# Weights' loads moved, the first lists' stores on another queue, and an addition in place of identity products, in a graph network of four layers

## The chip, the cores and the metric

The kernel runs on one core of a Trainium2 chip. A core has five engines with an instruction stream each: PE (TensorE, matrix products), DVE (VectorE), ACT (ScalarE), POOL (GpSimd) and SP (SyncE, which here only starts DMAs). Every stream is worked off in its written order. DMAs are started by SP and by POOL; sixteen DMA engines move the data. The metric is the device time of one execution in microseconds, as the median of several runs; it was 3134.76 us before (three runs, 3123.56 to 3135.57).

## The reference

Eight batches of a graph with 2048 nodes and 128 features go through four layers over one adjacency matrix (about 17 neighbours a node; the lists have room for 40). Layers 0 and 2 are attention with eight heads of 16, then a feed-forward part; layers 1 and 3 are graph attention with one score per edge:

```python
# layers 0 and 2
scores = jnp.einsum('bnhd,bmhd->bhnm', Q, K) / jnp.sqrt(HEAD_DIM)
scores = jnp.where(adj == 0, -jnp.inf, scores)
x = layer_norm(h + softmax(scores) @ V @ Wo + bo)
x = layer_norm(x + relu(x @ W1 + b1) @ W2 + b2)
# layers 1 and 3
e = leaky_relu(s_i[:, :, None] + s_j[:, None, :])
x = layer_norm(softmax(where(adj == 0, -inf, e)) @ (x @ W) + x)
```

All is in float32. The softmax runs over a node's neighbours only, and the kernel uses that.

## The kernel before, in words

**Tiling.** The nodes are cut into 32 units of 64 nodes. For each layer a *table* lies in memory: one row for each node, with keys and values (attention) or projected features (graph attention) of all eight batches. For each unit the kernel gathers the rows of all its edges, nine gathers of 128 rows, in five steps (two gathers in a step, one in the last), into one of six `kv` buffers. In an attention layer PE spreads each node's query over its edges (`qe`, L1484), DVE multiplies it with the gathered keys (L1496) and sums by head (L1503), ACT takes the exponential, POOL (sometimes DVE) weighs the values (L1522), and PE adds up by node (L1550). Then follow the output product, the norms, the feed-forward part, and the projection of the new features into the next layer's table.

**The start.** Three things run side by side. *Table 0*: `load` (L1188) brings features of four units at a time from memory into a `kv` buffer, `project` (L1280) multiplies by `Wkv` on PE (`ps_p`, L1295), ACT or DVE copies into one of three row buffers, and two DMAs store a unit's rows (L1343). No gather of layer 0 starts before the whole table is stored. *The lists*: `block_list` (L996) reads 128 rows of the adjacency, and DVE finds each node's neighbours in order; `unit_list` (L1076) then makes, for each unit, the list that says which node sits in which slot. ACT writes one-hot columns into a `hot` buffer (three passes, L1104 to L1108), PE multiplies with them so that each slot receives its node's neighbours, degree and offset (`ps_l`, L1117), and a second product with the identity adds the slot's own number in the same accumulation (L1124, the constant `place`). DVE picks from this the neighbour (L1133 to L1151), ACT writes the gather's indices, and the `hot` buffer is stored to memory as `hots[u]` (L1174), from where every layer's `fetch` (L1216) reads it again (L1230), into one of the same three `hot` buffers. *Weights*: `fill` (L909) loads each weight (L915); bias columns are loaded one element to a partition. The list of a unit leads its use by `LEAD`, twelve units of five steps.

**Order.** Nothing here is ordered by hand. `Plan` (L574) gets each operation with an assumed cost, the engines that may do it, what it reads and writes, and a key that says how soon it is due; a list scheduler replays this with a fixed number of buffers for each kind of tile and writes out one order per engine. A layer's keys start at `n * STRIDE`; weights have the key `n * STRIDE - 900`, the first `Wkv` -3000, the features for table 0 `u - 1500`, lists `10 * i - LEAD`. What an operation waits for at run time is what stands before it on its own engine, and the data and buffers it needs. DMAs of SP pass through eight completion counters in turn, so that a DMA also waits for the eighth one before it on this queue.

Of the kernel before, what the change touches and what calls it, by code (L numbers as in the profile page):

```python
# [9 lines left out]
F32 = mybir.dt.float32  # L10
# [5 lines left out]
ALU = mybir.AluOpType  # L16
# [724 lines left out]
class Sparse:  # L741
# [15 lines left out]
    def __init__(self, ctx, tc, x, xt, adj, w, out):  # L757
        self.tc, self.nc, self.w, self.xt_in, self.out = tc, tc.nc, w, xt, out
        self.B, self.N, _ = x.shape
        self.NB = self.N // P  # L760
        self.NU = self.N // UNIT
        self.HB = self.B // 2

        def pool(name, **kw):
            return ctx.enter_context(tc.tile_pool(name=name, **kw))

        self.nc.scalar.preload_act_table_set("natural_log_exp_and_others")
        self.const = pool("const", bufs=1)
        self.dram = pool("dram", bufs=1, space=DRAM)
        self.plan = Plan(self.nc)  # L770
        self.op, self.cell = self.plan.op, self.plan.cell
        for tag, bufs in SBUF_BUFS.items():
            self.plan.pool(tag, pool(f"sb_{tag}", bufs=bufs), bufs, tag in BY_KEY)
        for tag, bufs in PSUM_BUFS.items():
            self.plan.pool(tag, pool(f"ps_{tag}", bufs=bufs, space=PSUM), bufs)

        self.constants()
        self.weights_at = [Cell() for _ in LAYERS]
        self.keys_at = Cell()
        self.gates = {}  # L780
        self.layers = [
            self.mha_weights(n) if kind is MHA else self.gat_weights(n)
            for n, kind in enumerate(LAYERS)
        ]


        self.tables = [
            self.dram.tile([self.N, self.B * (2 * P if kind is MHA else P + 1)], F32, name=f"table_{n}")
            for n, kind in enumerate(LAYERS)
        ]  # L790
        self.table = [Cell() for _ in LAYERS]

# [23 lines left out]
    def constants(self):  # L816
# [23 lines left out]
                allow_small_or_imprecise_dtypes=True,  # L840
            )
        self.rank = ramp("rank", [P, DEG], [[1, DEG]])
        self.place = const.tile([P, TG, 2, DEG + 2], F32, name="place")
        nc.gpsimd.memset(self.place, 0.0)
        for j in range(2):
            nc.gpsimd.iota(
                self.place[:, :, j, DEG],
                pattern=[[P, TG]],
                base=0,
                channel_multiplier=1,  # L850
                allow_small_or_imprecise_dtypes=True,
            )
        nc.gpsimd.iota(
            self.place[:, TG - 1, 1, DEG : DEG + 1],
            pattern=[[1, 1]],
            base=GS - 1,
            channel_multiplier=-1,
            allow_small_or_imprecise_dtypes=True,
        )
        self.place = self.place.rearrange("p t j c -> p t (j c)")  # L860
        self.target = ramp("target", [P, GROUP], [[1, GROUP]], base=1)
        self.falling = const.tile([P, self.N], F32, name="falling")
        nc.gpsimd.iota(
# [45 lines left out]
    def fill(self, n, *pairs, at=None):  # L909

        for t, a in pairs:

            def start(e, t=t, a=a):
                with self.nc.allow_non_contiguous_dma(reason="a small array, once"):
                    e.dma_start(out=t, in_=a)  # L915

            self.op({"SP": 0.45}, start, -3000 if at else n * STRIDE - 900, joins=[at or self.weights_at[n]], dma=P * P * 4)

    def column(self, n, name, width=1):
        t = self.const.tile([P, width], F32, name=f"{name}_{n}")  # L920
# [3 lines left out]
    def mha_weights(self, n):  # L924
        const, w = self.const, self.w[n]
        d = {}
        for name, shape in (("Wq", [P, P]), ("Wkv", [P, 2 * P]), ("Wo", [P, P]), ("W1", [P, FFN])):
            d[name] = const.tile(shape, F32, name=f"{name}_{n}")
        d["W2"] = const.tile([P, FFN // P, P], F32, name=f"W2_{n}")
        self.fill(  # L930
            n, (d["Wkv"][:, 0:P], w["Wk"]), (d["Wkv"][:, P : 2 * P], w["Wv"]), at=None if n else self.keys_at
        )
        self.fill(
            n,
            (d["Wq"], w["Wq"]),
            (d["Wo"], w["Wo"]),
            (d["W1"], w["W1"]),
            (d["W2"], w["W2"].rearrange("(c p) m -> p c m", p=P)),
        )
        d["b1"] = self.column(n, "b1", FFN // P)  # L940
        for name in ("bo", "ln1_g", "ln1_b", "b2", "ln2_g", "ln2_b"):
            d[name] = self.column(n, name)
        return d
# [132 lines left out]
    def unit_list(self, u, p, block_aux, key):  # L1076
# [37 lines left out]
        def parts(e):  # L1114
            for t in range(TG):
# [3 lines left out]
                    lhsT=hot.tile[:, t * P : (t + 1) * P],  # L1119
                    rhs=aux.tile.rearrange("p j c -> p (j c)"),  # L1120
                    start=True,
                    stop=False,
                )
                e.matmul(out, lhsT=self.ident, rhs=self.place[:, t], start=False, stop=True)  # L1124

        op({"PE": 1.6}, parts, key, reads=[hot, aux], writes=[ps_l])
        rank = cell("rank_e", [P, TG, 2])
        pick = cell("pick", [P, TG, 2, DEG])
        shape = [P, TG, 2, DEG]


        def sources(e):
            e.tensor_tensor(  # L1133
                pick.tile,
                self.rank.unsqueeze(1).unsqueeze(1).to_broadcast(shape),
# [2 lines left out]
            )  # L1138
            e.tensor_tensor(pick.tile, pick.tile, ps_l.tile[:, :, :, 0:DEG], ALU.mult)

        op({"DVE": 1.2}, sources, key + 0.4, reads=[ps_l], writes=[pick])

        def ones(e):
            shape = [P, TG, 2, GROUP]
# [12 lines left out]
        def indices(e):  # L1157
# [12 lines left out]

        op({"ACT": 1.2}, indices, key - 2, reads=[rank, ps_l], writes=[self.idx_at[u], both])
        op(
            {"SP": 0.45},
            lambda e: e.dma_start(out=self.hots[u], in_=hot.tile),  # L1174
            key,
            reads=[hot],
# [39 lines left out]
    def fetch(self, n, u, key):  # L1216
# [3 lines left out]
            {"SP": 0.45},  # L1220
            lambda e: e.dma_start(out=x.tile, in_=self.xd[u] if n else self.xt_in[u]),
            key,
            reads=[self.x_at[u]] if n else [],
            writes=[x],
            dma=P * CH * 4,
        )
# [53 lines left out]
    def project(self, n, u, x, key, of=None, shares=()):  # L1280
# [6 lines left out]
        for v in range(2):  # L1287
# [12 lines left out]

            self.op({"PE": 1.1 if mha else 0.7}, products, key, reads=[x, self.keys_at if n == 0 else self.weights_at[n]], writes=[ps], holds=[rows], shares=shares)
            if n == 0:
                self.gates[u] = ps
            if mha:
                self.op(
                    {"ACT": 0.6, "DVE": 0.65} if n == 0 else {"ACT": 0.6},
# [33 lines left out]
        def store(e):  # L1340
# [2 lines left out]
                e.dma_start(out=self.tables[n][nodes, hf * half : (hf + 1) * half], in_=rows.tile[part])  # L1343

        self.op(
            {"SP": 0.9} if n else {"SP": 0.9, "POOL": 1.3}, store, key, reads=[rows], joins=[self.table[n]], dma=P * hb * width * 4
        )

    def norm(self, r, key):
# [502 lines left out]
    def run(self, adj):  # L1852
# [6 lines left out]
                self.load(u, ring)  # L1859
        for i in range(self.NB):  # L1860
            self.block_list(adj, i)
        for n, kind in enumerate(LAYERS):
            if kind is MHA:
                self.attention(n)
            else:
                self.graph(n)
        self.plan.issue()

    def failed(self):
# [72 lines left out]
```

## Time and profile before

| | before |
|---|---|
| median of three runs | 3134.76 us |
| the profiled execution, its own time | 3401.39 us |
| its span | 3399.6 us |
| PE busy / mean granted clock | 2640.6 us (78%) / 0.854 |
| DVE busy | 2190.5 us (64%) |
| ACT busy | 1381.2 us (41%) |
| POOL busy | 2130.8 us (63%) |
| DMA | 1088 MB, mean 320 GB/s |

The profiled execution is slower than the timed ones; times inside it are to be compared with its own span. Busy time says little alone, because the layers have different limits: layer 0 lasts until about 1190 us of the span, layer 1 until about 1870, layer 2 until about 2720. In what follows, an instruction is named by its line, engine, and the tiles it writes and reads (`kv<-qe,kv`); in a timeline the bracket gives the idle time before it and what ended it. The "granted clock" is the share of full speed that PE had.

### The profile page before, as it was taken

What the parts mean: (1) busy time and instruction counts of PE and PEld (TensorE: products, weight loads), DVE (VectorE), ACT (ScalarE), POOL (GpSimd) and SP (SyncE); (2) the same over time, 40 slices, a digit from 0 to 9 for tenths busy, and PEclk for the clock granted to TensorE, in tenths of its full rate; (3) what the DMA queues carried; (4) which work ended last, traced back from release to release, by engine and by line L of the source; (5) the groups of instructions that cost most, each with busy time, mean ns of one, the idle gap of its engine ahead of it and who ended that gap; (6) DMA issues with size and microseconds to landing.
All of it is one profiled execution on the core that took longest, in us unless ns stands there. A gap on an engine that the chain in (4) does not pass through costs nothing.

```text
span 3399.6 us, 69398 instructions
## 1 busy us (share of the span) xinstructions
PE 2640.6 (78%) x26600; PEld 1609.8 (47%) x26600; DVE 2190.5 (64%) x3384; ACT 1381.2 (41%) x4753; POOL 2130.8 (63%) x1452
## 2 busy tenths in 40 slices
PE   6877878888888758778886788888888866777775
PEld 5744444444433336666665333334333335556554
DVE  3778988987887713333333989889988833444434
ACT  3534544545444333333434244444444442333223
POOL 0157877877888834444552878888878835555442
PEclk8778988998999878888888889999999986777676
DMA  7868989988898859998997999999999949899885
GB/s 259 318 236 349 360 313 368 353 335 331 341 344 331 307 196 321 328 335 308 331 341 229 370 340 381 393 367 377 379 356 358 374 166 325 309 320 318 289 281 161
DMA packets 271637, 1088.01 MB, mean 320 GB/s; under 512 B 41217, under 2 KB 59905, under 8 KB 199393
## 3 DMA queue, kind: packets, MB, share of 16 engines
q0 software_dynamic: 166048, 861.26, 67.6%
q1 hardware_dynamic: 105248, 222.23, 18.6%
q8 instruction: 213, 3.49, 0.4%
q14 instruction: 128, 1.04, 0.1%
HBM read 1031.29 MB, written 99.75 MB: 333 GB/s over the span
## 4 chain that ended last, share of the span: by engine, by line
PE 29%; DMA 13%; DVE 11%; issue 11%; POOL 5%; another core or an unknown queue 4%; ACT 3%; ACTq 0%; SPq 0%; DVEq 0%; POOLq 0%
DMA kv<-table,idx 12%; PE acc L1773 6%; DVE kv L1496 5%; PE acc_q L1773 5%; PE ps_c L1262 3%; POOL kv L1522 3%; PE qe L1484 3%; PE ps_te L1651 2%; PE acc L1550 2%; POOL kv L1411 2%; PE ps_p L1295 2%; DVE s L1503 2%; PE ps_t L1250 1%; ACT junk L1358 1%
## 5 line engine op out<-in xcount | busy, mean ns | idle before, releaser
L1411 POOL DMA_INDIRECT kv<-table,idx x1152 | 1180.0, 1024 | 1118.1 <-issue 346.7
L1522 POOL TENSOR_TENSOR kv<-kv 128x2048 f32<-128x2048 f32 (+1 forms) x264 | 943.0, 3583 | 100.8 <-ACT kv L1513 95.2
L1496 DVE TENSOR_TENSOR kv<-qe,kv 128x2048 f32<-128x2048 f32 (+1 forms) x320 | 663.0, 2072 | 156.7 <-DMA kv<-table,idx 110.4
L1503 DVE TENSOR_REDUCE s<-kv 128x128 f32<-128x2048 f32 (+1 forms) x320 | 660.0, 2063 | 7.7
L1484 PE MATMUL qe<-q_sb,hot 32*128 32x512 f32 (+1 forms) x2304 | 398.3, 697 | 170.1 <-DVE kv L1496 155.6
L1773 PE MATMUL acc<-kv,w 128*32 128x128 f32 x5120 | 300.4, 336 | 160.1 <-issue 90.3
L1550 PE MATMUL acc<-kv,hot 128*32 128x512 f32 x2560 | 362.6, 644 | 48.1 <-POOL kv L1522 41.7
L1746 DVE TENSOR_TENSOR w<-hot,e 128x512 f32<-128x512 f32 (+1 forms) x384 | 222.7, 600 | 247.4 <-ACT e L1736 85.3
L1773 PE MATMUL acc_q<-kv,w 128*32 128x128 f32 x5120 | 268.0, 321 | 82.5 <-issue 64.4
L1773 PEld LDWEIGHTS acc<-kv,w 128*32 128x32 f32 x5120 | 190.3, 133 | 245.5 <-issue 156.3
L1513 ACT ACTIVATE kv<-s 128x128 f32<-128x128 f32 (+1 forms) x320 | 95.7, 299 | 406.4 <-DVE s L1503 285.4
L1773 PEld LDWEIGHTS acc_q<-kv,w 128*32 128x32 f32 x5120 | 179.4, 127 | 147.7 <-issue 112.0
L1484 PEld LDWEIGHTS qe<-q_sb,hot 32*128 32x128 f32 (+1 forms) x2304 | 106.8, 197 | 291.3 <-DVE kv L1496 217.6
L1358 ACT ACTIVATE junk<-ps_c,eps 128x128 f32<-128x128 f32 x512 | 187.7, 367 | 113.1 <-PE ps_c L1262 94.7
L1736 ACT ACTIVATE e<-e 128x16 f32<-128x16 f32 (+1 forms) x320 | 66.6, 212 | 316.2 <-DVE e L1731 169.7
L1550 PEld LDWEIGHTS sums<-kv,hot 128*32 128x32 f32 x2560 | 87.7, 116 | 210.8 <-issue 203.8
L1380 ACT ACTIVATE normed<-ps_c,rstd 128x128 f32<-128x128 f32 x512 | 163.4, 366 | 2.4
L1272 PE MATMUL ps_f<-x,W 128*128 128x512 f32 x256 | 148.8, 669 | 18.5 <-ACT x L1397 11.1
L1262 PE MATMUL ps_c<-centre,r 128*128 128x128 f32 x1024 | 148.5, 290 | 18.3 <-DVE kv L1522 9.5
L1262 PEld LDWEIGHTS ps_c<-centre,r 128*128 128x128 f32 x1024 | 127.3, 196 | 71.0 <-DVE r L1587 31.8
L1358 ACT ACTIVATE junk<-r,eps 128x128 f32<-128x128 f32 x256 | 103.2, 403 | 121.1 <-DVE r L1822 92.9
L1250 PE MATMUL ps_t<-ident,normed 128*128 128x128 f32 x640 | 128.1, 329 | 27.5 <-DVE kv L1522 12.1
(156 smaller groups left out, 3992.9 us busy)
## 6 DMA issues: line engine op xcount, KB each, us to landing
hot<-hots SPq DMA_DIRECT2D x128, 480.0 KB
table<-trows SPq DMA_DIRECT2D x126, 256.0 KB
xd<-xnew SPq DMA_DIRECT2D x96, 256.0 KB
x<-xd SPq DMA_DIRECT2D x96, 256.0 KB
kv<-table,idx POOLq DMA_INDIRECT x1152
table<-trows SPq DMA_DIRECT2D x128, 129.0 KB
kv<-adj_dram SPq DMA_DIRECT2D x16, 1024.0 KB
hots<-hot SPq DMA_DIRECT2D x32, 480.0 KB
```

The lines of the kernel that those rows point to most:

```text
L1250: e.transpose(ps.tile[:, b * P : (b + 1) * P], flat(x.tile)[:, b * P : (b + 1) * P], self.ident)
L1262: e.matmul(ps.tile[:, cols], lhsT=flat(x.tile)[:, cols], rhs=self.centre, start=True, stop=True)
L1358: e.activation(self.junk, flat(r.tile)[:, b * P : (b + 1) * P], AF.Square, bias=self.eps, scale=P**-0.5, accum_out=var.tile[:, b : b + 1],)
L1380: lambda e, b=b: e.activation(normed.tile[:, b, :], flat(r.tile)[:, b * P : (b + 1) * P], AF.Copy, scale=rstd.tile[:, b : b + 1],),
L1411: e.indirect_dma_start(out=rows(kv.tile, j), out_offset=None, in_=self.tables[n], in_offset=bass.IndirectOffsetOnAxis(ap=self.idx[:, u, co ...
L1484: e.matmul(qe.tile[:, j, hf, :], lhsT=hot.tile[rows, t * P : (t + 1) * P], rhs=q.tile[rows, :], start=True, stop=True,)
L1496: e.tensor_tensor(k, qe.tile[:, 0:tiles].rearrange("p j h c -> p (j h) c"), k, ALU.mult)
L1503: e.tensor_reduce(s.tile[:, 0 : tiles * heads].rearrange("p (q c) -> p q c", q=2 * tiles), k, axis=mybir.AxisListType.X, op=ALU.add,)
L1522: e.tensor_tensor(v, v, w.unsqueeze(3).to_broadcast([P, 2 * tiles, heads // 2, HD]), ALU.mult)
L1550: e.matmul(out[rows, :], lhsT=hot.tile[:, col : col + GROUP], rhs=rhs[:, 2 * (j % tiles) + hf, :], start=(t == 0), stop=(t == TG - 1),)
L1746: e.tensor_tensor(w.tile[:, j : j + tiles], oh[:, j : j + tiles].unsqueeze(2).to_broadcast(shape), e8.tile[:, 0:tiles].unsqueeze(3).to_bro ...
L1773: e.matmul(acc()[rows, b * P : (b + 1) * P], lhsT=w.tile[:, j, hf * hb + b, :], rhs=both_rows(kv)[:, j % tiles, hf * hb + b, 0:P], start=F ...
```

## The change

The change has four parts.

1. *Weights.* Only `Wkv` of layer 0 is asked for at the start. The other weights of layer 0 read a *gate*: they cannot be planned before the projections of unit 16 are done, those of layer 1 before unit 24's, those of later layers before unit 8 of an earlier layer is stored. The features for layer 0's queries wait for unit 20. `gates` holds cells that no longer keep a tile alive.
2. *Lists' stores.* The `hots` store of the first twelve units goes to POOL's DMA queue; later ones stay on SP's.
3. *Table stores of layer 0.* All on SP; POOL may no longer take them.
4. *Slots' numbers.* `place` shrinks from 84 to 2 columns a tile; the second product with the identity is gone, and DVE adds `place` to one column of `ps_l` in PSUM, ahead of its other work on the list.

```diff
-        self.layers = [
-            self.mha_weights(n) if kind is MHA else self.gat_weights(n)
-            for n, kind in enumerate(LAYERS)
-        ]
+        self.gate = self.keys_at
+        keys = self.const.tile([P, 2 * P], F32, name="Wkv_0")
+        self.fill(0, (keys[:, 0:P], w[0]["Wk"]), (keys[:, P : 2 * P], w[0]["Wv"]), at=self.keys_at)
+        self.layers = [{"Wkv": keys}]
...
-        self.place = const.tile([P, TG, 2, DEG + 2], F32, name="place")
-        nc.gpsimd.memset(self.place, 0.0)
+        self.place = const.tile([P, TG, 2], F32, name="place")
...
-            self.op({"SP": 0.45}, start, -3000 if at else n * STRIDE - 900, joins=[at or self.weights_at[n]], dma=P * P * 4)
+            self.op(
+                {"SP": 0.45},
+                start,
+                -3000 if at else n * STRIDE - 900,
+                reads=[] if at else [self.gate],
+                joins=[at or self.weights_at[n]],
+                dma=P * P * 4,
+            )
...
                     start=True,
-                    stop=False,
+                    stop=True,
                 )
-                e.matmul(out, lhsT=self.ident, rhs=self.place[:, t], start=False, stop=True)
-        op({"PE": 1.6}, parts, key, reads=[hot, aux], writes=[ps_l])
+        op({"PE": 0.8}, parts, key, reads=[hot, aux], writes=[ps_l])
...
         def sources(e):
+            e.tensor_tensor(ps_l.tile[:, :, :, DEG], ps_l.tile[:, :, :, DEG], self.place, ALU.add)
...
-        op({"DVE": 1.2}, sources, key + 0.4, reads=[ps_l], writes=[pick])
+        op({"DVE": 1.3}, sources, key + 0.4, writes=[pick, ps_l])
...
         op(
-            {"SP": 0.45},
+            {"POOL": 0.75} if u < LEAD // TG else {"SP": 0.45},
             lambda e: e.dma_start(out=self.hots[u], in_=hot.tile),
...
-            reads=[self.x_at[u]] if n else [],
+            reads=[self.x_at[u] if n else self.gates[20]],
...
             if n == 0:
-                self.gates[u] = ps
+                self.gates[u] = Cell()
+                self.gates[u].writers = list(ps.writers)
...
-            {"SP": 0.9} if n else {"SP": 0.9, "POOL": 1.3}, store, key, reads=[rows], joins=[self.table[n]], dma=P * hb * width * 4
+            {"SP": 0.9}, store, key, reads=[rows], joins=[self.table[n]], dma=P * hb * width * 4
...
         for i in range(self.NB):
             self.block_list(adj, i)
+        self.gate = self.gates[16]
+        self.layers[0] = self.mha_weights(0)
+        self.gate = self.gates[24]
         for n, kind in enumerate(LAYERS):
+            if n + 1 < len(LAYERS):
+                more = self.mha_weights if LAYERS[n + 1] is MHA else self.gat_weights
+                self.layers.append(more(n + 1))
             if kind is MHA:
                 self.attention(n)
             else:
                 self.graph(n)
+            self.gate = self.x_at[8]
         self.plan.issue()
```

In the order that the planner writes for the changed kernel, SP's first table stores stand right after the first loads of features and adjacency; layer 0's other weights stand among the stores of about the 16th to 19th unit, layer 1's about five units later; unit 0's list is loaded right after the last table store; and eight lists' stores stand in POOL's stream ahead of the first gather, four more among the gathers of the first units.

More of the change, by code (lines that the diff above doesn't have):

```diff
@@ L842, in constants @@
         self.rank = ramp("rank", [P, DEG], [[1, DEG]])
-        self.place = const.tile([P, TG, 2, DEG + 2], F32, name="place")
-        nc.gpsimd.memset(self.place, 0.0)
+        self.place = const.tile([P, TG, 2], F32, name="place")
         for j in range(2):
             nc.gpsimd.iota(
-                self.place[:, :, j, DEG],
+                self.place[:, :, j],
                 pattern=[[P, TG]],
@@ L853, in constants @@
         nc.gpsimd.iota(
-            self.place[:, TG - 1, 1, DEG : DEG + 1],
+            self.place[:, TG - 1, 1:2],
             pattern=[[1, 1]],
@@ L859, in constants @@
         )
-        self.place = self.place.rearrange("p t j c -> p t (j c)")
         self.target = ramp("target", [P, GROUP], [[1, GROUP]], base=1)
@@ L927, in mha_weights @@
         for name, shape in (("Wq", [P, P]), ("Wkv", [P, 2 * P]), ("Wo", [P, P]), ("W1", [P, FFN])):
-            d[name] = const.tile(shape, F32, name=f"{name}_{n}")
+            if n or name != "Wkv":
+                d[name] = const.tile(shape, F32, name=f"{name}_{n}")
         d["W2"] = const.tile([P, FFN // P, P], F32, name=f"W2_{n}")
-        self.fill(
-            n, (d["Wkv"][:, 0:P], w["Wk"]), (d["Wkv"][:, P : 2 * P], w["Wv"]), at=None if n else self.keys_at
-        )
+        if n:
+            self.fill(n, (d["Wkv"][:, 0:P], w["Wk"]), (d["Wkv"][:, P : 2 * P], w["Wv"]))
+        else:
+            d["Wkv"] = self.layers[0]["Wkv"]
         self.fill(
```

## The prediction

> **What bounds the kernel now.** I read the stages first (busy time by stretch, cut at the two events below), because the change touches only the start and the first layer: the instruction order of before and after is the same on every engine from about 1000 us on. Columns: stretch, length, busy us of PE, weight loads, DVE, ACT, POOL, granted clock, DMA share, GB/s.
>
> ```profile
> 0.00:140.00 140.00, 100.38 (x461) 83.08 (x461) 78.79 (x273) 59.58 (x146) 7.74 (x36) 0.83 0.82 269
> 140.00:175.00 35.00, 24.36 (x110) 23.73 (x110) 15.17 (x58) 16.98 (x58) 10.98 (x11) 0.51 0.96 382
> 175.00:205.00 30.00, 23.37 (x134) 13.84 (x137) 23.18 (x19) 10.58 (x34) 12.12 (x5) 0.61 0.26 93
> 205.00:300.00 95.00, 72.15 (x518) 36.44 (x510) 82.04 (x97) 38.97 (x124) 73.72 (x39) 0.86 0.80 309
> ```
>
> Until 140 us table 0 is written and no engine is full. Then the gathers fill the DMA engines for 35 us while DVE is 43% busy, and after that DMA is nearly idle: the gathered rows lie there and nobody multiplies them. Next the timelines of SP, PE, POOL and DVE (start, length, engine, line, idle before):
>
> ```profile
> 20.66 0.43 SPq L915 DMA_DIRECT2D ln_b<-L_ln_b_dram  x1
> 21.14 1.39 SPq L1221 DMA_DIRECT2D x<-xt_dram  x3
> 22.64 1.16 SPq L1343 DMA_DIRECT2D table<-trows  x2
> ...
> 23.96 2.05 PE L1445 MATMUL ps_q<-Wq,x 128*128 128x128 f32 x8 [9.37 <-DMA x<-xt_dram]
> ...
> 135.73 0.59 SPq L1343 DMA_DIRECT2D table<-trows  x1
> ...
> 140.76 1.07 POOL L1411 DMA_INDIRECT kv<-table,idx  x1 [126.61 <-DMA hots<-hot]
> ...
> 170.54 0.32 SPq L1230 DMA_DIRECT2D hot<-hots  x1
> ...
> 179.17 2.29 DVE L1496 TENSOR_TENSOR kv<-qe,kv 128x2048 f32<-128x2048 f32 x1 [0.39 <-PE qe L1484]
> ...
> 189.43 2.29 DVE L1496 TENSOR_TENSOR kv<-qe,kv 128x2048 f32<-128x2048 f32 x1 [0.88 <-PE qe L1484]
> ```
>
> Two faults of order. At 5 to 21 us SP holds eleven weight loads before the first table store, and PE waits 9.4 us for the first x. At 136 us the last table store is out and the gathers start 5 us later, but the list of unit 0 that the first product needs (L1230) stands on SP behind the stores of the fifth to ninth lists, and is issued at 170.5. SP's waits from 136 to 180 us (total, times, longest):
>
> ```profile
> SPq L1174 <- DVE hot L1145: 24.2, 4, 9.1
> SPq L1174 <- DVE pick L1139: 12.3, 1, 12.3
> ```
>
> So 36.5 us of waits in SP's queue stand between table and first product; 38.4 us pass from first gather to first multiply. Last the slots' numbers, and DVE's waits in layer 0 (205 to 1000 us):
>
> ```profile
> L1124 PE MATMUL ps_l<-place,ident x320: 275/275/423, 61.7 to 850.9; 128*128 128x84 f32 x160
> ...
> DVE pick L1133 <- PE ps_l L1124: 16.1, 9, 3.8
> ...
> L1331 DVE TENSOR_TENSOR t<-ps_p,strip 128x8 f32<-128x8 f32 x46 | 7.4, 161 | 18.4 <-ACT trows L1320 12.7 <-PE ps_p L1297 5.6
> ```
>
> **What the Trainium skill says.** "Perfetto Trace Analysis", section on the HWDGE DMA instruction: the semaphore wait is taken by the issuing sequencer before it does anything else, so what stands behind waits too; the 36.5 us agree. "DMA: Bandwidth & Descriptors", "Issuing engines are not separate DMA queues": another issuing engine saves sequencer time, not bandwidth; so I credit POOL's stores with order alone. Same page, "Rules for kernel authors": a strided last dimension becomes one descriptor per element. The bias columns are that: 2337 of 8083 packets in the first 60 us are under 512 B. They are moved, not removed.
>
> **The change part by part**, against the profiled execution (3401.4 us, span 3399.6). It is 8.5% above the median of the three runs, 3134.8; I scale by 0.922 at the end.
>
> 1. *Weights later.* Eleven loads leave the head of SP's queue and stand among the table stores of about units 16 to 19; five of layer 1 follow. SP time is the same (16 x 0.43 = 7 us) and so are the packets. The gain: PE does not stop at 14.6 us with full row buffers; the fourth unit is copied when the first store lands, about 18 us (5 MB of loads stand before it, at the 358 to 423 GB/s of these slices) and not 27.8: at most 10 us. DMA gives a second bound. It was busy 0.82 x 140 = 115 us before the first gather; 3 to 4 more lists' stores now come first (1.7 MB at 400 GB/s, 4 us), so 119 us; at a share of 0.90 that is 133 us, at 0.96 124, at 0.84 142. I take **first gather at 133, -8 us** (-17 to +1).
>
> 2. *First twelve lists' stores on POOL.* SP's queue runs from the last table store straight to unit 0's list. What then comes last is the list work: after the last projection the products of two lists are left before the first spread of queries, where before five were. On PE and ACT they go as a pair: split 2.0 us, six target passes of 0.83 (5.0), ten products 4.3 at half clock, the spread 2.1, a few hops: 14 to 18 us after the last projection, which leads the gather by 5. So first multiply about 13 us after the first gather, at 146 and not 179.2: with step 1's 8, **this part gives 25 us** (20 to 30). The gathers land by then: two MB at 400 GB/s take 5 us. POOL pays 12 issues of 0.65 (the row of its two table stores, half the rows) to 1.02 us (a gather): 8 to 12 us. Eight fall in its 126.6 us of idleness; four stand between gathers, 3 to 4 us, covered by the wait for buffers, to be paid whole if that cover goes.
>
> 3. *No identity products.* 160 products go, 0.22 us apart at full clock, 0.43 at half: 1.1 or 2.15 us a list. In the start this is in step 2. Between first and second multiply 10.3 us pass, most of it for a list's ten products at half clock; now no list stands there, and the pace is the gathers' 5.2 us: **-5**. In layer 0 the nine waits of DVE (16.1 us) can lose up to 1.1 us each, I take half: -5 (0 to -10).
>
> 4. *The addition on DVE.* 32 instructions of 128x10 on PSUM. Nearest row 0.161 us (128x8, one operand in PSUM); "VectorE: DVE Perf Modes", section on the errata, gives 120 + 10 cycles at 0.96 GHz, 0.135 us as an estimate; the row decides. 22 lie in layer 0, where DVE is the fullest engine: **+3.6** (0 to +4). The weight centring of layer 1 (four instructions, 0.9 us, and a copy of 0.3) moves there too: +1.3.
>
> 5. *Small ones at nothing.* First table stores from POOL to SP: two issues of 0.6 us, behind loads that must land anyway. x of the first queries after the 20th unit: PE wants it five units later, about 15 us. Layers 2 and 3's weights keep their places at the layers' ends. One memset less on POOL, 0.45 us, idle there.
>
> Sum: -8 -25 -5 -5 +5 = -38 us of 3401; x 0.922 = -35. **3100 us.**
>
> **Rivals.**
> A, *the start shrinks further* (-55 to -80 us): the stores, no longer behind lists, let DMA run at 0.96 or more, as it did from 80 to 110 us (0.98), and the granted clock, 0.5 from 140 to 195, recovers as PE no longer waits. First gather 122, multiply 134, layer 0 gains 10: -62 x 0.922 = -57: 3078. Against: the store path itself waited (ACT for row buffers, 24.4 us in nine waits) and stays.
> B, *the prologue gives nothing and layer 0 takes back* (-3 to -20 us): the weights' small packets now compete with table stores, gather at 141; -25 -5 +5 +6 for a worse interleaving = -19, x 0.922 = -17: 3117. For: layer 0's DMA runs at 0.80 to 0.93, and the head start of 11 gathered MB that the late multiply had is gone.
> C, *slower: the wait moves to POOL.* The first gather now stands in POOL's queue behind the store of the eighth list. Before, that store went out at 162.7 us. If the eighth list is no earlier, gathers start at 164, the multiply at 176, and the last four stores hold later gathers too: +8 for those, +5 for DVE, -3: +10 x 0.922: 3144. It decides when the eighth list ends after about 166 us. Against: the sixth to eighth lists' products now stand before the end of the projections, each list is 2 us shorter, and the eighth should end some 5 us after the last projection.
> D, *nothing*: gather 150 and multiply 163: -16 +3: inside the bound.
>
> **How the numbers follow.** Forecast 0.60 (own range 3085 to 3117), A 0.14, B 0.14 (a third of it under 0.5%), D 0.07, C 0.05. Half a per cent, about what a measurement of this kernel can tell from no change, is 15.7 us: faster below 3119. Forecast and A 0.74, two thirds of B 0.09: faster 0.82 with rounding down; same 0.12; slower 0.06. Leaving out the far halves of A, and of C with D's end, gives 3066 to 3128.
>
> **What would show it.** Right: SP issues its first table stores before 15 us; no PE wait for x near 24; unit 0's list is issued within 5 us of the last table store; first gather 124 to 142, first multiply within 18 us of it, the second 4 to 7 later; DMA above 0.7 where it was 0.26; additions of 0.15 to 0.17 us; 160 fewer products. Wrong: POOL waiting for DVE's list before its first gather (C); the last table store after 140 us (B); the first multiply waiting for ACT's targets or a list buffer more than 20 us after the gather; layer 0 longer than before from its first multiply to its end.

## The result, and the profile after

The changed kernel took 3109.44 us (median of six runs, 3101.04 to 3119.12) beside 3134.34 us for the kernel before (six runs, 3123.56 to 3144.61): a ratio of 0.9939, 95% interval 0.9914 to 0.9963, or 25 us less. The forecast was 3100 us, 35 us less. Its profiled execution took 3110.49 us with a span of 3108.4 us.

First the stages of the changed kernel, cut at the same times and with the same columns as before (busy us of PE, weight loads, DVE, ACT, POOL; granted clock; DMA share; GB/s):

```profile
0.00:140.00 140.00, 100.06 (x410) 78.39 (x410) 83.57 (x284) 63.78 (x162) 10.54 (x41) 0.83 0.80 273
140.00:175.00 35.00, 25.34 (x111) 17.88 (x112) 27.74 (x70) 14.94 (x53) 16.18 (x15) 0.50 0.95 363
175.00:205.00 30.00, 21.21 (x137) 10.48 (x136) 27.23 (x25) 10.85 (x32) 24.50 (x14) 0.67 0.81 307
205.00:300.00 95.00, 78.20 (x565) 38.09 (x568) 88.05 (x117) 46.61 (x153) 79.01 (x43) 0.92 0.90 356
```

The hole is closed: from 175 to 205 us the DMA share is 0.81, where it was 0.26. DVE is busy for 27.74 of the 35 us from 140 us on, where it was 15.17. The first stretch, until 140 us, is hardly different.

Then the timelines of SP, PE, POOL and DVE of the changed kernel (start, length, engine, line; in brackets the idle time before it and what ended it):

```profile
13.16 5.63 SPq L1354 DMA_DIRECT2D table<-trows  x6
...
20.31 1.13 PE L1305 MATMUL ps_p<-Wkv,kv 128*128 128x256 f32 x4 [2.53 <-ACT trows L1250]
...
117.42 23.85 SPq L1354 DMA_DIRECT2D table<-trows  x14
...
131.68 2.36 PE L1126 MATMUL ps_l<-unit_aux,hot 128*128 128x84 f32 x20
...
137.78 1.75 PE L1305 MATMUL ps_p<-Wkv,kv 128*128 128x256 f32 x4 [3.74 <-ACT empty L1178]
...
142.18 0.34 SPq L1240 DMA_DIRECT2D hot<-hots  x1
...
145.20 1.06 POOL L1422 DMA_INDIRECT kv<-table,idx  x1 [5.51 <-PE ps_off L1073]
...
154.79 2.29 DVE L1507 TENSOR_TENSOR kv<-qe,kv 128x2048 f32<-128x2048 f32 x1 [0.60 <-DMA kv<-table,idx]
...
162.01 2.28 DVE L1507 TENSOR_TENSOR kv<-qe,kv 128x2048 f32<-128x2048 f32 x1
```

The first table store stands at 13 us and PE's wait for the first features is gone, as forecast. But the first gather is at 145.2 us, not at 133: it is later than before (140.76). What came forward is the other end: unit 0's list is loaded at 142 us and not at 170.5, and the first multiply stands at 154.8 us and not at 179.2, 9.6 us behind the first gather.

The middle of this timeline tells why the gather is late. At 131.7 us PE makes the products of the seventh and the eighth list in one go (20 of them), and the last projection, behind them, waits 3.74 us. ACT L1178 is the last reader of a list's products, so what the projection waits for is the PSUM tile that they hold.

Last the products of the lists, and what DVE waited for in layer 0 (205 to 1000 us; total, times, longest):

```profile
L1126 PE MATMUL ps_l<-unit_aux,hot x320: 236/276/510, 47.4 to 818.3; 128*128 128x84 f32 x160
L1141 DVE TENSOR_TENSOR ps_l<-ps_l,place x32: 165/168/177, 49.9 to 820.2; 128x10 f32<-128x10 f32 x32
...
DVE kv L1507 <- DMA kv<-table,idx: 42.0, 26, 4.3
...
DVE ps_l L1141 <- PE ps_l L1126: 5.6, 6, 1.5
```

The identity products are gone (the products with the one-hot columns remain, 320 records; the row of the identity products, also 320, no longer exists). DVE waits 5.6 us for lists' products and waited 16.1; it waits 42.0 us for gathered rows and waited 33.4.

### The profile page after: what moved, and what is told of

It reads as the page before. It is cut to its first block, busy times and chain, and to the rows that moved or that the text cites. A ratio compares the mean times of both kernels' runs of the same rounds, so it can differ in the third digit from the quotient of the medians.

```text
span 3108.4 us, 68763 instructions
## 1 busy us (share of the span) xinstructions
PE 2430.9 (78%) x26280; PEld 1492.3 (48%) x26280; DVE 2209.2 (71%) x3420; ACT 1383.4 (45%) x4749; POOL 2128.5 (68%) x1461
## 5 line engine op out<-in xcount | busy, mean ns | idle before, releaser
L1784 PE MATMUL acc<-kv,w 128*32 128x128 f32 x5120 | 224.0, 331 | 104.7 <-DVE w L1757 103.8
L1735 DVE TENSOR_TENSOR e<-te,kv 128x16 f32<-128x16 f32 (+1 forms) x320 | 58.2, 182 | 303.8 <-DMA kv<-table,idx 290.8
L1784 PE MATMUL acc_q<-kv,w 128*32 128x128 f32 x5120 | 209.1, 309 | 58.3 <-DVE w L1757 57.7
L1784 PEld LDWEIGHTS acc<-kv,w 128*32 128x32 f32 x5120 | 168.4, 133 | 135.1 <-DVE w L1757 116.1
L1784 PEld LDWEIGHTS acc_q<-kv,w 128*32 128x32 f32 x5120 | 158.7, 124 | 85.4 <-DVE w L1757 68.9
```

Of the source, the lines that this page charges most:

```text
L1784: e.matmul(acc()[rows, b * P : (b + 1) * P], lhsT=w.tile[:, j, hf * hb + b, :], rhs=both_rows(kv)[:, j % tiles, hf * hb + b, 0:P], start=F ...
```

## The experiments

Twelve runs were made, two of them repetitions (of the kernel before and of the changed one). Each ratio is to the kernel before on the same chip. "Weights later" always includes the change's third part, the table stores of layer 0 all on SP; in the kernels without it just two of the 64 table stores, at about 13 us, stand on POOL. The two parts were not separated. The first question was whether SP's queue (theory Q, the prediction's step 2) or the chain of the lists with its few buffers (theory L) sets the first multiply, and what the weights (theory W) and the addition do alone. The table gathers what the timelines and stages showed; "15th list" is the time at which PE makes that list's products, "DVE" its busy time in the first 205 us (all in us).

| kernel | first gather | unit 0's list loaded | first multiply | 15th list | DVE | ratio (95%) |
|---|---|---|---|---|---|---|
| before, again | 139.6 | 166.6 | 176.9 | 290 | 118.9 | 0.9994 (0.9974 to 1.0014) |
| stores on POOL only | 139.6 | 175.4 | 180.7 | 290 | 117.8 | 1.0017 (1.0001 to 1.0033) |
| weights later only | 145.2 | 169.6 | 182.6 | 295 | 115.7 | 1.0022 (1.0004 to 1.0039) |
| addition only | 148.0 | 163.0 | 180.5 | 286 | 118.5 | 1.0045 (1.0029 to 1.0061) |
| without stores on POOL | 142.1 | 142.1 | 154.1 | 264 | 139.1 | 0.9920 (0.9900 to 0.9941) |
| without weights later | 150.2 | 177.9 | 188.0 | 304 | 112.5 | 1.0080 (1.0061 to 1.0100) |
| without the addition | 137.3 | 166.4 | 176.1 | 293 | 119.1 | 1.0008 (0.9992 to 1.0025) |
| change, lists 7 to 10 held back | 137.4 | 155.2 | 165.8 | 283 | 133.5 | 1.0003 (0.9989 to 1.0016) |
| before, last projection held back | 164.3 | 161.1 | 177.2 | 293 | 119.1 | 0.9977 (0.9961 to 0.9993) |
| addition, last projection held back | 164.0 | 163.9 | 175.8 | 293 | 122.3 | 1.0019 (1.0005 to 1.0033) |
| change, again | 140.6 | 137.3 | 150.2 | 265 | 141.5 | 0.9928 (0.9898 to 0.9958) |
| without stores on POOL, other PSUM tile | 138.1 | 139.3 | 157.5 | 266 | 139.3 | 0.9925 (0.9904 to 0.9947) |

The kernels with a ratio near 0.993 are those with the early first multiply, and in them the lists are ahead later on, too: PE makes the 15th list's products at 264 to 266 us, in all others at 283 to 304.

### The kernel before, once more

No edit. Expected:

> The kernel before, once more, for a second trace: in the first one the two graph layers moved data at about 330 GB/s where the changed kernel's moved 400, with the same instructions in the same order. If that was the one execution and not the kernel, the new span is about 3130 us, its layer 1 runs at about 400 GB/s, and its first 200 us look as before: first gather at 139 to 142 us, first multiply at 176 to 180. If the changed kernel really speeds up the graph layers, the new span is near 3400 again and the timed ratio stays 1.00 all the same.

It took 3122.35 us in the timed runs, and its profile has a span of 3118.7 us, where the first profile of the same kernel had 3399.6. The stages of the two profiles tell where these 281 us lie; the first profile:

```profile
300.00:1200.00 900.00, 745.45 (x5292) 380.94 (x5292) 752.64 (x811) 423.81 (x1415) 703.98 (x379) 0.91 0.88 338
1226.00:1846.00 620.00, 483.57 (x7496) 374.15 (x7497) 203.19 (x735) 236.28 (x835) 295.21 (x288) 0.82 0.89 314
```

and the repetition:

```profile
300.00:1200.00 900.00, 745.35 (x5298) 375.57 (x5298) 748.79 (x806) 430.40 (x1434) 700.61 (x376) 0.92 0.88 338
1211.00:1720.00 509.00, 410.05 (x7495) 345.20 (x7495) 207.45 (x735) 236.93 (x834) 291.41 (x288) 0.83 0.98 382
```

The first rows are layer 0 and alike within 2% in every column. The second rows are layer 1: the same instructions in 620 us at 314 GB/s, or in 509 us at 382. Layer 0's last multiply (L1496) starts at 1184.5 us in the first profile and at 1168.3 in the second, so 16 of the 281 us lie up to there; most of the rest lies in layers 1 and 3. On one chip every run was later as slow as that profile: the kernel before took 3395 us there, and 3123 on two others. Why layers 1 and 3 are slower there isn't settled. For the prediction it means that its factor of 0.922 did not belong on a gain that lies in layer 0.

### Each part alone

Stores of the first twelve lists on POOL, on the kernel before:

```diff
-            {"SP": 0.45},
+            {"POOL": 0.75} if u < LEAD // TG else {"SP": 0.45},
             lambda e: e.dma_start(out=self.hots[u], in_=hot.tile),
```

> The kernel before with one part of the change: the first twelve lists' stores on POOL's queue. PE's order stays that of before, with five lists' products between the last projection and the first spread of queries. Theory Q (the prediction's: SP's queue held unit 0's list back): the list is loaded at about 142 us, the first multiply comes at 150 to 160, the time falls by 15 to 25 us. Theory L (the chain of lists on PE, ACT and DVE held it): the list is loaded early but the first multiply stays at 172 to 179, and the time changes by less than 6 us.

No gain: 1.0017. SP's queue is free of list stores up to the list of unit 0 here, and that list was loaded even later than before. Theory L has the time, but it too expected an early load, and the multiply, at 180.7 us, is just outside its range. The timeline:

```profile
164.42 0.57 POOL L1174 DMA_DIRECT2D hots<-hot  x1 [4.30 <-DVE rank_e L1151]
...
175.39 4.95 SPq L1230 DMA_DIRECT2D hot<-hots  x2
```

and the wait of SP from 136 to 180 us:

```profile
SPq L1230 <- DMA hots<-hot: 43.5, 2, 39.5
```

SP waited 39.5 us at the load itself, for a store out of a list buffer to land. "Perfetto Trace Analysis" of the Trainium skill (section on the HWDGE DMA instruction) was right that what stands behind a waiting DMA waits too; but the load waits for the same lists by its buffer, so taking it out from behind them moved the wait and did not remove it. Theory Q falls as a cause by itself. (A kernel with more list buffers, which would test that wait directly, was not run.)

Weights later (with the gates, and all table stores on SP), on the kernel before:

```diff
+        self.gate = self.gates[16]
+        self.layers[0] = self.mha_weights(0)
+        self.gate = self.gates[24]
```

> The kernel before with only the weights loaded later (with the gates, and table stores of layer 0 all on SP). Theory W (the stall at 15 to 26 us was a loss of the start): last table store 8 to 12 us earlier than before, at 124 to 128, first gather at 129 to 133, time down by 8 to 12 us. Theory L: the start is held by row buffers and by the lists woven in, so the last table store stays within 5 us of 136, the first multiply within 8 us of 179, and the time within 8 us.

1.0022. The first table store is early, but the last one ends at 141 us, the gather is at 145.2 and the multiply at 182.6. Theory W falls.

The addition in place of the identity products, on the kernel before:

```diff
-                e.matmul(out, lhsT=self.ident, rhs=self.place[:, t], start=False, stop=True)
+            e.tensor_tensor(ps_l.tile[:, :, :, DEG], ps_l.tile[:, :, :, DEG], self.place, ALU.add)
```

> The kernel before with only the slots' numbers added by DVE. Each list's products take half as long on PE. Theory L: with 2 us less a list and fewer lists behind the last projection, the first multiply comes 8 to 15 us earlier than 179, and the time falls by 6 to 15 us. Theory Q: the list of unit 0 stays behind the stores on SP, only each list is 2 us quicker, so at most -8 us at the first multiply, and DVE's additions give 3 to 4 us back: -5 to 0 us.

1.0045: slower, which no theory said. In its written order the planner leaves five lists' products behind the last projection, as before, and the last table store is at 144 us. Parts of which none gains alone gain 0.6% together: an interaction, so the next runs took one thing away from the whole.

### The change with one part taken away

The changed kernel with SP's list stores back:

```diff
-            {"POOL": 0.75} if u < LEAD // TG else {"SP": 0.45},
+            {"SP": 0.45},
```

> The changed kernel with the lists' stores back on SP's queue (weights later and the addition kept). In the written order PE has two lists' products after the last projection, as in the changed kernel. Theory L (what made the first multiply early is how few lists stand on PE between the last projection and the first spread): unit 0's list loaded at 142 to 150, first multiply 152 to 162, total 0.990 to 0.996 of before. Theory Q (the early multiply comes from SP's queue holding no list stores): unit 0's list at 160 or later, first multiply 170 or later, total 0.998 to 1.004. Theory I (two parts together are needed, order and queue): between, multiply 162 to 170.

0.9920, all of the gain. Its timeline:

```profile
133.56 2.07 PE L1304 MATMUL ps_p<-Wkv,kv 128*128 128x256 f32 x4 [3.75 <-ACT empty L1178]
...
142.05 1.15 POOL L1421 DMA_INDIRECT kv<-table,idx  x1 [134.63 <-DMA hots<-hot]
...
142.10 0.33 SPq L1239 DMA_DIRECT2D hot<-hots  x1
...
154.06 2.29 DVE L1506 TENSOR_TENSOR kv<-qe,kv 128x2048 f32<-128x2048 f32 x1 [3.76 <-DMA kv<-table,idx]
```

With the stores on SP the first multiply is as early as with them on POOL. The part to which the prediction gave 25 us is worth nothing that these runs can see.

The changed kernel with all weights at the start again (and two table stores on POOL again); of that edit:

```diff
-        self.gate = self.gates[16]
-        self.layers[0] = self.mha_weights(0)
-        self.gate = self.gates[24]
```

> The changed kernel with the weights loaded at the start as before (lists' stores on POOL and the addition kept). PE has the seventh to tenth lists' products after or among the last projections, as with the addition alone. Theory L: first multiply 168 to 182, total 1.000 to 1.006 of before. Theory Q: list loaded right after the last table store, first multiply by 160, total 0.992 to 0.997. Either way the PE wait for the first features near 24 us is back.

1.0080, the slowest kernel of the study. The gather is at 150.2 us and the multiply at 188.0, outside both theories' ranges. PE has five lists' products behind the last projection, and its wait for the first features (9.2 us, until 23.6) is back.

The changed kernel with the identity products back:

```diff
-            e.tensor_tensor(ps_l.tile[:, :, :, DEG], ps_l.tile[:, :, :, DEG], self.place, ALU.add)
+                e.matmul(out, lhsT=self.ident, rhs=self.place[:, t], start=False, stop=True)
```

> The changed kernel with the identity products back (weights later and POOL's stores kept). Four lists' double products stand on PE after the last projection, as with the weights alone. Theory L: list loaded 160 to 172, first multiply 172 to 185, total 0.998 to 1.004 of before. Theory Q: list at 142 to 150, first multiply 155 to 162, total 0.991 to 0.997.

1.0008, no gain. The table is early (gather at 137.3), but four lists' products stand behind the last projection, and the multiply comes at 176.1. These are theory L's numbers, as they were in the run without the stores. So the weights' part and the addition are both needed, and the lists' stores on POOL are not. In the changed kernel and in the one without its stores on POOL, and in no other so far, the written order has eight lists' products ahead of the last projection and two behind it.

### The order alone

The changed kernel, whole; only the planner may not place the products of the seventh to tenth lists before the last projection:

```diff
+        late = [self.gates[self.NU - 1]] if 6 <= u < 10 else []
-        op({"PE": 0.8}, parts, key, reads=[hot, aux], writes=[ps_l])
+        op({"PE": 0.8}, parts, key, reads=[hot, aux, *late], writes=[ps_l])
```

> The changed kernel, all three parts kept, but the products of the seventh to tenth lists may be planned only after the last projection (so four lists, not two, between it and the first spread). If those two lists ahead of the last projection are what lets the first multiply come early, the table ends earlier (last store at 131 to 138, first gather 135 to 142) but the list load slips to 150 or later and the first multiply to 162 to 178; total 0.996 to 1.003 of before. If they only delay the table (SP's queue being what counts), first gather 133 to 138, first multiply 143 to 150, total 0.988 to 0.993.

1.0003, with the first case's numbers: the whole gain is gone with one added dependence for the planner, while all parts of the change are in the kernel. Its timeline:

```profile
130.98 1.03 PE L1306 MATMUL ps_p<-Wkv,kv 128*128 128x256 f32 x4
...
132.95 2.44 PE L1126 MATMUL ps_l<-unit_aux,hot 128*128 128x84 f32 x20
...
137.37 1.07 POOL L1423 DMA_INDIRECT kv<-table,idx  x1 [28.15 <-issue]
...
155.15 20.27 SPq L1241 DMA_DIRECT2D hot<-hots  x2
...
165.75 2.29 DVE L1508 TENSOR_TENSOR kv<-qe,kv 128x2048 f32<-128x2048 f32 x1 [4.54 <-PE qe L1496]
```

The last projection no longer waits, and the gather is at 137.4 us, 3 to 8 us ahead of the changed kernel's two profiles. That bought nothing: the list of unit 0 is loaded 13 to 18 us later, and the first multiply comes 11 to 16 us later. Still it comes 11 to 13 us earlier than in the kernel before, and the total is the same as before. The stages say where this lead went. The kernel with lists held back:

```profile
0.00:205.00 205.00, 141.26 (x619) 103.32 (x623) 133.51 (x377) 87.47 (x242) 46.14 (x65) 0.76 0.81 284
205.00:380.00 175.00, 139.38 (x892) 69.26 (x885) 146.24 (x187) 74.28 (x242) 126.19 (x68) 0.80 0.80 307
```

and, on the same chip, the one without stores on POOL:

```profile
0.00:205.00 205.00, 147.34 (x671) 106.29 (x675) 139.06 (x381) 90.49 (x251) 46.03 (x58) 0.77 0.83 297
205.00:380.00 175.00, 142.43 (x1062) 70.14 (x1054) 163.67 (x203) 94.13 (x308) 146.68 (x80) 0.95 0.92 362
```

By 205 us DVE (the third number) has done 133.5 and 139.1 us of work, against 118.9 in the kernel before. From 205 to 380 us it does 163.7 us where the lists came early, 146.2 where they were held back (157.7 in the kernel before). The held-back kernel loses its lead there; the waits in its trace are many and small (no single one of DVE's or POOL's in this stretch is over 8 us), so which of them is the cause stays open.

How much of an early start is kept can be read from the first and the last of layer 0's 160 multiplies (count; shortest, median and longest in ns; start of the first and of the last). In this order: the kernel before in its repeated profile, the changed kernel in both profiles, the one without stores on POOL, the one with lists held back:

```profile
L1496 DVE TENSOR_TENSOR kv<-qe,kv x160: 1209/2281/2294, 176.9 to 1168.3; 128x2048 f32<-128x2048 f32 x128, 128x1024 f32<-128x1024 f32 x32
L1507 DVE TENSOR_TENSOR kv<-qe,kv x160: 1160/2283/2293, 154.8 to 1153.4; 128x2048 f32<-128x2048 f32 x128, 128x1024 f32<-128x1024 f32 x32
L1507 DVE TENSOR_TENSOR kv<-qe,kv x160: 1160/2282/2293, 150.2 to 1138.3; 128x2048 f32<-128x2048 f32 x128, 128x1024 f32<-128x1024 f32 x32
L1506 DVE TENSOR_TENSOR kv<-qe,kv x160: 1160/2283/2293, 154.1 to 1146.7; 128x2048 f32<-128x2048 f32 x128, 128x1024 f32<-128x1024 f32 x32
L1508 DVE TENSOR_TENSOR kv<-qe,kv x160: 1160/2282/2293, 165.8 to 1187.3; 128x2048 f32<-128x2048 f32 x128, 128x1024 f32<-128x1024 f32 x32
```

In these three profiles of kernels that gained, the lead of 22 to 27 us over the first line at the first multiply is 15 to 30 us at the last (19 and 10 us in the kernel with another PSUM tile below): the gain is made at the start and kept, within the 16 us by which the two profiles of the kernel before differ at that point. The held-back kernel is 12 us behind the one without stores on POOL at the first multiply and 41 us at the last, so most of its loss comes inside layer 0. Its written order of lists' products and spreads differs there as well. This run therefore shows that the planner's order decides the gain, not that the two early lists do it alone.

Then the reverse: nothing of the change, and only the last projection made to wait for the eighth list's products. First on the kernel before, then on the addition alone:

```diff
+        o = op({"PE": 1.6}, parts, key, reads=[hot, aux], writes=[ps_l])
+        if u == 7:
+            o.next.append(self.last)
+            self.last.waits += 1
```

> The kernel before with none of the change's parts; one dependence is added for the planner: the last projection of table 0 may be planned only after the eighth list's products. In the written order one list's products, not five, then stand on PE between the last projection and the first spread. Theory O (the order of lists and last projection on PE is the cause by itself): the table ends later (last store 142 to 150, first gather 146 to 154), unit 0's list is loaded within 8 us of that, first multiply 157 to 166, total 0.992 to 0.997 of before. Rival S (work must be saved: weights out of the way and ten products less a list): first multiply 172 or later, total 0.999 or more.

> The addition on VectorE alone, with the same dependence for the planner (last projection after the eighth list's products); the addition without it took 1.0045 of before. Theory O: first gather 146 to 152, first multiply 156 to 165, total 0.991 to 0.997. Rival S: first multiply 172 or later, total 1.001 or more. If the addition itself is worth something at a fixed order, this run is below the same dependence without the addition by 2 to 8 us.

0.9977 and 1.0019; the first multiply is at 177.2 and 175.8 us. Both miss theory O; rival S has both multiplies and the second ratio, not the first. The second was to be 2 to 8 us below the first if the addition is worth something at a fixed order; it is 16 us above it by the medians. So the addition shows no worth of its own here, though the two written orders also differ inside layer 0. The first of them, in its timeline:

```profile
156.54 1.99 PE L1299 MATMUL ps_p<-Wkv,kv 128*128 128x256 f32 x4
...
164.33 1.07 POOL L1416 DMA_INDIRECT kv<-table,idx  x1 [150.05 <-DMA hot<-hots]
...
177.16 2.28 DVE L1501 TENSOR_TENSOR kv<-qe,kv 128x2048 f32<-128x2048 f32 x1
```

Here the lists do not come earlier; the table comes later, up to where the lists are. The last projection is at 156.5 us and not at 133 to 138. So eight lists ahead of the last projection are not sufficient; the lists must also be ready sooner, which is read from the timelines and not tested by itself. In the kernels that gained, the eighth list's products are made at 128 to 133 us and the tenth's at 145 to 150; in the kernel before at 149 and 168, in this one at 152 and 171. The 7 us that the first of these two kernels gained remain unexplained: its profiled span, 3119.2 us, is that of the kernel before, while the median of its runs is 3114.01.

### The change once more, and an attempt at more

> The changed kernel once more, beside before on this chip: ratio 0.991 to 0.996 whatever the chip's own pace; first gather 143 to 147, first multiply 153 to 157. The changed kernel without its stores on POOL took 0.992 of before: if those stores are worth nothing, this run has the same ratio within its interval.

0.9928, 3101.78 us, the same as the first time within the intervals, and the same as without the stores on POOL. The first gather was at 140.6 us in this profile and at 145.2 in the first, so it moves by 5 us between two executions; gather and multiply are both earlier than was expected here. The gap from there to the first multiply was 9.6 us in both, and the second multiply came 7.2 us later in both.

Last, without stores on POOL, and with the last projection in the PSUM tile `sums`, which is free at that time:

```diff
+            tag = "sums" if n == 0 and (u, v) == (self.NU - 1, 1) else tag
```

> Weights later and the addition, lists' stores on SP, and the last projection of table 0 takes its PSUM tile from the buffer named sums, which is free there, in place of one of the two that the seventh and eighth lists hold. If that buffer is what the last projection waits 3.7 us for, this wait goes, the last table store and the first gather come 3 to 5 us earlier than in the changed kernel (first gather 137 to 142), and the first multiply 0 to 4 us earlier (150 to 154); total 0.988 to 0.993. If the wait is only moved (row buffers or ACT), first gather 142 or later and 0.991 to 0.996.

```profile
128.35 2.36 PE L1126 MATMUL ps_l<-unit_aux,hot 128*128 128x84 f32 x20
130.55 1.06 PE L1305 MATMUL ps_p<-Wkv,kv 128*128 128x256 f32 x4
...
138.12 1.63 POOL L1422 DMA_INDIRECT kv<-table,idx  x1 [130.70 <-ACT empty L1178]
...
157.51 2.28 DVE L1507 TENSOR_TENSOR kv<-qe,kv 128x2048 f32<-128x2048 f32 x1
```

This settles what the 3.7 us were: with another tile the last projection follows the lists at once, and the gather is at 138.1 us. The total stays (0.9925). In this order the planner put layer 1's weight centring ahead of the first spread, and the multiply came at 157.5 us. The earlier end of the table brought no earlier multiply in this order. No kernel of the study beats the changed one by more than the intervals; the two without stores on POOL equal it.

## Why the prediction was right, and where it was wrong

The time (3109 us, forecast 3100, range 3066 to 3128) and the direction were right, and so was the idea that a first multiply some 25 us earlier shortens the whole by about as much. Of the steps, the largest has the right size with the wrong cause, one failed, and two sizes were off. That the sum came out near the result is in part luck: step 1 gave nothing, and the gain of step 2 came from other parts than the one it was given to.

**Step 1, weights later, failed as a gain.** The early part of it happened: six table stores were issued before 20 us where the kernel before had two, and 18 by 40 us where its two profiles have 12 and 13. But this lead of five or six was two or three at 50 us, four to six at 70, and two at 90 (counted in the timelines). The first gather came at 140.6 and 145.2 us, not at 133, where the two profiles of the kernel before have 139.6 and 140.8; rival B had said 141. The step took DMA's busy time as the bound. What took the lead at 50 us stays open. From 65 to 80 us the weights' loads now stand among the table stores (read from the timeline, not tested by itself), and the last 3.7 us went at the tile that the lists' products hold (tested). Three kernels with the first gather at 137 to 138 us were no faster for it.

**Step 2, the stores on POOL, had the right size and the wrong cause.** It forecast 13 us from gather to multiply (9.6 measured) and the multiply at 146 us (150.2 and 154.8; before 176.9 and 179.2). It gave this to SP's queue. Part of the 36.5 us that it read there could not hold the list back: some 7 us are the wait of the store at 178.4 us, which stands behind the list's load at 170.5. Alone that part cost 4 us, and the change without it has the whole gain. The fact under the step was right, though: "the products of two lists are left before the first spread of queries, where before five were". It appears in the written order, and it comes from the weights' part and the addition together.

**Step 3, no identity products,** forecast -5 us between first and second multiply (10.3 to 5.2; measured 7.2, and 8.4 in the repeated profile of the kernel before) and -5 us in layer 0. There DVE's wait for lists' products fell from 15.4 (in the repeated profile) to 5.6 and 4.2 us, so by 10 to 11, the far end of its range. What the step did not see is that, with the weights later, their absence lets the planner bring the lists forward: with them back the eighth list's products stand at 145 us, 12 to 17 us later than in the changed kernel, and the gain is zero.

**Step 4, the addition,** was forecast at 0.161 us; it took 0.168 (median), 32 times, 5.5 us in all. The estimate from "VectorE: DVE Perf Modes" of the Trainium skill (section on the errata), 0.135 us, was too low for a sum with one operand and the result in PSUM. The same section has a formula for a float32 `tensor_tensor` addition, (N + 151) cycles at 0.96 GHz, which the page checked at 512 and 2048 elements; for N = 10 it gives an estimate of 0.168 us, and the trace agrees.

**The scale** of 0.922 was wrong: the slow first profile was slow almost only behind layer 0. Unscaled the sum says -38 us, 3097.

**What layer 0 took back.** The first multiply is 22 to 29 us earlier, and with step 3's rest and the addition some 30 us should remain by the prediction's own terms. The medians differ by 25 and 21 us. Rival B named a place where the rest could go, the lost head start of gathered rows, at +6 us. The same waits in the repeated profile of the kernel before read:

```profile
DVE kv L1496 <- DMA kv<-table,idx: 36.4, 21, 5.2
DVE pick L1133 <- PE ps_l L1124: 15.4, 9, 3.8
```

DVE's wait for gathers in layer 0 is 42.0 and 46.3 us in the changed kernel's two profiles, 36.4 and 33.4 in those of the kernel before; but it is 31.9 in the kernel without stores on POOL, which gained as much. So this wait does not explain the rest, which stays open. The prediction's sign against it, a layer 0 that is longer from first to last multiply, did not appear: 999 and 988 us against 1005 and 991.

Rival A did not happen (first gather 122 forecast; the granted clock from 140 to 175 us stayed at 0.50), and rival C neither: POOL waited 26.8 us for a list, but its eighth store went out at 139 us, ahead of the end of the table, not at 162.7.

## What to carry to other kernels

When a planner writes the order, price a change by the order that it produces and not by the line that was edited: here two parts, each useless alone, together let the lists run two ahead, and a third that looked like the cause did nothing that could be measured. A wait in a queue is worth removing only if the waiting instruction does not need the same thing by its buffer. And a start is not shortened at its last-named wait: ask which engine has idle time early and is full later (DVE here), and whether the change lets it use that time. The kernel with lists held back shows that this alone is not enough: DVE had done 15 us more work than before by 205 us, and the order behind it lost that again.

## What the runs showed of the hardware

The same program ran at two paces: the kernel before took 3395 us on one chip and 3123 on two others, and two of its profiles, of 3399.6 and 3118.7 us, have layer 0 alike within 2% and layer 1 at 314 or 382 GB/s; the change without its stores on POOL had 0.992 on the slow one, the whole change 0.993 on one of the others. In the kernel with stores on POOL only, the last list's store ahead of unit 0's list was issued among gathers at 164.4 us, and the list's load, which waited for a list's store to land, started 11 us later, at 175.4. This is no rule: with the identity products back, in the same place, 2.7 us lay between (163.7 and 166.4). An addition of 128x10 on VectorE with one operand and the result in PSUM took 0.165 to 0.177 us.
